# Layer 0 of a two-layer kernel: the queries join the seven products of half blocks, row sums come from DRAM, and the norm's unrotated weights move to the turned keys

## The chip, the cores and the metric

The kernel runs on one core of a Trainium2 chip. A core has five engines that each run their own instruction stream in order: TensorE (PE in the profile, with its weight loads as PEld), VectorE (DVE), ScalarE (ACT), GpSimd (POOL) and SyncE (SP, here only issuing transfers). The metric is the time of one execution on the device in microseconds. Before the change the median of three runs is 2171.02 us (2167.05 to 2172.69).

## The reference

The program is a small two-layer network on 4 sequences of 512 tokens with 512 features, all in 32-bit floats. Each layer normalises its input and adds an attention and a mixture of experts to it. The change concerns the attention of layer 0, which has 16 heads of 128 features:

```python
q = rope(rmsnorm(xn @ Wq + bq, qn_w))            # per head: 128 features
lk = rope(rmsnorm(xn @ Wlk + blk, kn_w))
lv = xn @ Wlv + blv
# sparse part: every 4 tokens are one compressed entry (ck, cv); top 8 of 128
sc = q @ ck.T * scale, causal;  ctx_sparse = softmax over the top 8 @ cv
# local part: window of 128 tokens back
ctx_local = softmax(q @ lk.T * scale, band) @ lv
out = merge_heads(0.5 * (ctx_sparse + ctx_local)) @ Wo + bo
```

`rmsnorm(x, w)` is `x * rsqrt(mean(x*x) + 1e-6) * w` over the 128 features of a head. `rope` rotates the first 64 features of a head by angles that depend on the token's place in its sequence, and leaves the other 64 as they are. The three products with `Wq`, `Wlk` and `Wlv` are each 2048 x 512 by 512 x 2048.

## The kernel before

**Loops.** The attention of layer 0 runs in 32 steps, written `for i, (g, b) in enumerate(steps)`: 8 groups `g` of two heads, and within each the 4 sequences `b`. Step i computes scores and context of its two heads, and between these it projects the queries, keys and values of step i + 1 (`project(i + 1)`). A step is 512 tokens, four blocks of 128 rows. Below these 32 steps are called loops 0 to 31. Loop 31 has nothing to project.

**Other work in the loops.** `run0((i, place))` lets other work in at five places of every loop: layernorm and routing in loops 0 to 4; the 39 expert blocks of layer 0 in loops 5 to 24 (`Experts.turn` transposes a block of gathered rows, tile `trm_r`, L382, with an ACT copy to `xT`, L384; `Experts.apply` multiplies it by the expert's weights, tile `hp_r`, L392, evicts on DVE, L394, and stores to DRAM, `yd`, through SP); the combination of the experts' rows in loops 24 to 28; the layernorm of layer 1 in loops 29 to 31.

**Projection.** Before the change the queries are plain products: `queries0(t)` (L554, tile `pq`) multiplies two row blocks by `Wq` in four steps of 128 features, 256 columns each. It is called twice a loop, for rows 0-255 and rows 256-511. Keys and values of the group together are one product of a 2 x 2 block matrix, computed by seven half-size products instead of eight (a Strassen form; `product`, L524, tile `p`): rows are split at 256, features at 256, and the outputs are keys and values. It needs sums of blocks of rows (`sums_x`, on DVE, tiles x1 to x3) and sums of weight blocks (`combine_weights`, once a group). `first_keys` makes p1 and p2, `second_keys` p6, p7 and p4, `values0` p5 and p3. Each product is a tile of 128 x 512 in PSUM: two row blocks of 256 columns.

**Norm and rotation.** `rope` (L427 to L448) runs on a block of 256 rows and 2 heads, that is four columns of sums `ss`, of queries or of keys. ACT squares and sums each of the four (L432), POOL adds epsilon (L434, L436) and raises to the power of -1/2 (L437), DVE rotates (L440 to L443), and for the queries ACT scales (L447, four copies). For the keys the scale is left to the exponential of the scores (`norm_k`, L613). `back()` turns the result with four PE transposes (tile `trq`, L543) and one ACT copy into `qkT` (L544). `t1` and `t2` hold cosines and sines times the norm weights, for all 128 features.

**Scores and context.** `scores` (L594 to L627) computes the sparse scores `sp` and local scores `st` on PE, the exponentials on ACT, the band mask on POOL (L617), and the top 8 on DVE. `turn` transposes the sparse weights (tile `trs`, L635, copies to `sT` on ACT, L637). `context` computes local and sparse context of one head into three PSUM tiles `ca`, `cb` and `cc` (L651, L653, L657), then on DVE the reciprocals of the sums (L660, L663), on ACT `half`, the sparse part scaled (L668, four copies), and on DVE `ctx`, the two parts added (L670, first from `cb`, then three from `ca`). `turn_context` (L677, L678) turns it into `cT`, and `output` (L685, L688) multiplies by `Wo` and adds to `acc`.

**PSUM.** `psum(tag, name)` gives banks of 128 x 512 floats in rotation: three for `mm` (projections, outputs, experts), three for `sc` (scores, context) and two for `tr` (transposes). A tile's first write waits until all reads of the bank's previous tile are done.

**Order.** The order in which the source states the work, and a scheduler that keeps each engine busy by its own estimates, set each engine's instruction order when the kernel is built. On the chip every engine runs its stream in that order. In loops 5 to 23 before the change PE runs: `op` of the loop before, scores of head 0, `pq`, p1 and p2, `trm_r`, scores of head 1, `trs`, `hp_r`, p6 and p7, `trq`, p4, `trq`, context of head 0, `trs`, `pq`, `trm_r`, `trq`, context of head 1, `trc`, `hp_r`, p5 and p3, `trq`, `trc`, `op`.

The loop's calls of the projection are these:

```python
back_q0, back_k0 = queries_a(), keys_a()
...
back_k1 = keys_b(back_q0)
ctx0 = context(i, 0, lT0, sT0, lv)
back_q1 = queries_b()
ctx1 = context(i, 1, lT1, sT1, lv)
values_()
```

Of the kernel before, what the change touches and what calls it, by code (L numbers as in the profile page):

```python
# [12 lines left out]
F32 = mybir.dt.float32  # L13
# [19 lines left out]
HG = 2  # L33
# [11 lines left out]
def two_layers(ctx: ExitStack, tc: tile.TileContext, a: dict, out: bass.AP, large: bass.AP):  # L45
# [29 lines left out]
    def load_group(g, between=None):  # L75
        cols = slice(g * HG * D, (g + 1) * HG * D)
        bqk = wpool.tile([P, 2, HG * D], F32, tag="bqk", name=f"bqk_{g}")
        bvg = wpool.tile([P, HG * D], F32, tag="bvg", name=f"bvg_{g}")
        ws = []
        for nm in ("Wq", "Wlk", "Wlv"):  # L80
            w = wpool.tile([P, KC, HG * D], F32, tag=nm, name=f"{nm}_{g}")
            nc.sync.dma_start(out=w, in_=a[nm][:, cols].rearrange("(k p) c -> p k c", p=P))
            ws.append(w)
            if nm == "Wq":
                for nm_, dst in (("bq", bqk[:, 0, :]), ("blk", bqk[:, 1, :]), ("blv", bvg)):
                    nc.sync.dma_start(out=dst, in_=a[nm_][cols].partition_broadcast(P))
            if between:
                between(nm)
        return ws, bqk, bvg
# [6 lines left out]
    def combine_weights(g):  # L96


        (_, w_k, w_v), bqk, bvg = groups[g]
        k1, k2, v1, v2 = w_k[:, 0:2, :], w_k[:, 2:4, :], w_v[:, 0:2, :], w_v[:, 2:4, :]  # L100
        t2_, t3_, t4_ = (wpool.tile([P, 2, HG * D], F32, tag=f"wT{x}", name=f"wT{x}_{g}", bufs=1) for x in (2, 3, 4))
        tc.keep_in_program_order(V.tensor_tensor(t3_, v2, v1, ALU.subtract))
        tc.keep_in_program_order(V.tensor_tensor(v1, v1, k1, ALU.subtract))
        tc.keep_in_program_order(V.tensor_tensor(t2_, v2, v1, ALU.subtract))
        tc.keep_in_program_order(V.tensor_tensor(t4_, t2_, k2, ALU.subtract))
        tc.keep_in_program_order(V.tensor_tensor(bvg, bvg, bqk[:, 1, :], ALU.subtract))
        sums_w[g] = t2_, t3_, t4_
# [14 lines left out]

    nw = wk0.tile([P, 2, D], F32, tag="s", name="nw")
    cos = wk0.tile([P, TC + 1, D], F32, tag="lT", name="cos")
    sin = wk0.tile([P, TC + 1, D // 2], F32, tag="lT", name="sin")

    def load_between(nm):
        if nm == "Wq":
            load_x(1)
        if nm == "Wlk":  # L130
            nc.sync.dma_start(out=nw[:, 0, :], in_=a["qn_w"].partition_broadcast(P))
            nc.sync.dma_start(out=nw[:, 1, :], in_=a["kn_w"].partition_broadcast(P))
            nc.sync.dma_start(out=cos, in_=a["c_cos"])
            nc.sync.dma_start(out=sin, in_=a["c_sin"])
            for n in range(2, TC):
                load_x(n)

    load_x(0)
    groups = {0: load_group(0, load_between)}
# [32 lines left out]
    t1 = const0.tile([P, TC + 1, 2, D], F32, tag="t1", name="t1")  # L172
    t2 = const0.tile([P, TC + 1, 2, D // 2], F32, tag="t2", name="t2")

    def tables():

        wmax = small.tile([P, 2], F32, tag="wmax", name="wmax")
        tc.keep_in_program_order(V.tensor_reduce(wmax, nw, AX.X, ALU.max, apply_absolute_value=True))
        V.tensor_tensor(wmax[:, 0:1], wmax[:, 0:1], wmax[:, 1:2], ALU.mult)
        V.tensor_scalar(wide, wmax[0:1, 0:1], LIMIT / math.sqrt(D), None, ALU.is_gt)  # L180


        for w in range(2):

            tc.keep_in_program_order(V.tensor_scalar(nw[:, w, :], nw[:, w, :], math.sqrt(D), None, ALU.mult))
            tc.keep_in_program_order(G.tensor_tensor(
                t1[:, :, w, :], cos, nw[:, w, :].unsqueeze(1).to_broadcast([P, TC + 1, D]), ALU.mult
            ))
            for half, other in ((0, 1), (1, 0)):
                G.tensor_tensor(  # L190
                    t2[:, :, w, ts(half, 32)],
                    sin[:, :, ts(half, 32)],
                    nw[:, w, ts(other, 32)].unsqueeze(1).to_broadcast([P, TC + 1, 32]),
                    ALU.mult,
                )
# [223 lines left out]
    lv = const0.tile([P, TC, HG, D + 1], F32, tag="lv", name="lv")  # L419
# [6 lines left out]
    def rope(qb, tt1, tt2, n, inner, pool, name, scale=True):  # L426


        sq = pool.tile([P, D], F32, tag="sq", name=f"sq_{name}", bufs=1)
        ss = small.tile([P, n], F32, tag="ss" if scale else "ssk", name=f"ss_{name}", bufs=3 if scale else 4)  # L430
        for h in range(n):
            A.activation(sq, qb[:, h, :], AF.Square, accum_out=ss[:, h : h + 1])  # L432
        if scale:
            G.tensor_scalar(ss, ss, D * 1e-6, None, ALU.add)  # L434
        else:
            G.tensor_scalar(ss, ss, D * 1e-6, float(D), ALU.add, ALU.mult)  # L436
        G.tensor_tensor(ss, ss, nhalf[:, 0:n], ALU.pow)  # L437
        r1 = pool.tile([P, n, D], F32, tag="r1", name=f"r1_{name}", bufs=2 if n > 1 else 1)
        r2 = pool.tile([P, n, D // 2], F32, tag="r2", name=f"r2_{name}", bufs=1)
        V.tensor_tensor(inner(r1), inner(qb), tt1, ALU.mult)  # L440
        V.tensor_tensor(inner(r2[:, :, 0:32]), inner(qb[:, :, 32:64]), tt2[0], ALU.mult)
        V.tensor_tensor(inner(r2[:, :, 32:64]), inner(qb[:, :, 0:32]), tt2[1], ALU.mult)
        V.tensor_tensor(r1[:, :, 0:64], r1[:, :, 0:64], r2, ALU.add)  # L443
        if not scale:
            return r1, ss
        for h in range(n):
            A.activation(r1[:, h, :], r1[:, h, :], AF.Copy, scale=ss[:, h : h + 1])  # L447
        return r1  # L448

    def compress(b, pool):  # L450
# [27 lines left out]
        for i, w in enumerate((wk, wv)):  # L478
            for k in range(KC):
# [5 lines left out]
        r = rope(ck, t1[:, TC, 1:2, :], (t2[:, TC, 1:2, 0:32], t2[:, TC, 1:2, 32:64]), 1,  # L485
                 lambda t: t, pool, f"ck_{b}")
        yield
        tr = psum("tr", f"trck_{b}")
        PE.transpose(tr[:, 0:C], r[:, 0, :], ident)
        A.copy(ckT[:, b, :], tr[:, 0:C])  # L490
# [7 lines left out]
    norm_k = {}  # L498

    def project(i):  # L500
# [4 lines left out]
        (w_q, w_k, w_v), bqk, bvg = groups[g]  # L505
        qkT = qp.tile([P, 2 * HG, S], F32, tag="qkT", name=f"qkT_{g}_{b}")
        x11, x12, x21, x22 = (xnT[:, ts(f, 2), ds(b * S + t * 256, 256)] for t in range(2) for f in range(2))
        half = [P, 2, 256]
        keep_ = {}

        def tmp(tag):
            keep_[tag] = wk0.tile(half, F32, tag=tag, name=f"{tag}_{i}", bufs=1)
            return keep_[tag]

        def sums_x():
            V.tensor_tensor(tmp("x3"), x11, x21, ALU.subtract)
            V.tensor_tensor(tmp("x1"), x21, x22, ALU.add)
            V.tensor_tensor(tmp("x2"), keep_["x1"], x11, ALU.subtract)

        def product(nm, x, w):  # L520
            p = psum("mm", f"{nm}_{i}").rearrange("p (c d) -> p c d", c=2)
            for c in range(2):
                for k in range(2):
                    PE.matmul(p[:, c, :], lhsT=x[:, k, ts(c, P)], rhs=w[:, k, :], start=(k == 0), stop=(k == 1))  # L524
            return p

        def finish(qb, w_, t):

            nm = f"{i}_{w_}_{t}"
            r = rope(  # L530
                qb.rearrange("p c (h d) -> p (c h) d", h=HG),
                t1[:, ts(t, 2), w_, :].unsqueeze(2).to_broadcast([P, 2, HG, D]),
                [t2[:, ts(t, 2), w_, ts(i_, 32)].unsqueeze(2).to_broadcast([P, 2, HG, 32]) for i_ in range(2)],
                2 * HG, lambda x: x.rearrange("p (c h) d -> p c h d", c=2), wk0, nm, scale=(w_ == 0),
            )
            if w_ == 1:
                r, norm_k[(i, t)] = r

            def back():
                tr = psum("tr", f"trq_{nm}")  # L540
                for h in range(HG):
                    for c in range(2):
                        PE.transpose(tr[:, ts(h * 2 + c, P)], r[:, c * HG + h, :], ident)  # L543
                A.copy(qkT[:, ts(w_, HG), ts(t, 256)], tr.rearrange("p (h t) -> p h t", h=HG))  # L544
            return back

        def rows_(nm):
            return wk0.tile(half, F32, tag="qb", name=f"qb_{nm}_{i}")

        def queries0(t):  # L550
            pq = psum("mm", f"pq_{i}_{t}").rearrange("p (c d) -> p c d", c=2)
            for c in range(2):
                for k in range(KC):
                    PE.matmul(pq[:, c, :], lhsT=xnT[:, k, ds(b * S + (2 * t + c) * P, P)], rhs=w_q[:, k, :],  # L554
                              start=(k == 0), stop=(k == KC - 1))
            qb = rows_(f"q{t}")
            V.tensor_tensor(qb, pq, bqk[:, 0, :].unsqueeze(1).to_broadcast(half), ALU.add)
            return finish(qb, 0, t)

        def first_keys():  # L560
# [1242 lines left out]
```

## Time and profile before

| | |
|---|---|
| median of three runs | 2171.02 us (2167.05 to 2172.69) |
| profiled execution | 2168.7 us |
| its span (first to last instruction) | 2166.8 us |
| granted TensorE clock, mean | 0.993 |
| PE, DVE, ACT, POOL busy | 2108.3, 1458.9, 848.4, 687.0 us |
| one loop with an expert (474 to 521 us) | 47.0 us |
| one loop without experts (1426.7 to 1467.7 us) | 41.0 us |

The profile is of one execution. Busy time is the time in which an engine runs at least one counted instruction. A line of a timeline gives start and duration in us, the engine, the line of the source, the operation, the tile written and those read, the shapes, and how many instructions the line joins; in brackets stand the idle time of the engine before it, and what ended it. A line of the chain of waits gives start, duration and what the run's end waited for at that time. A float32 matmul is two instructions in the profile: `x16` on L554 is eight products.

### The profile page before, as it was taken

How to read it: one execution, taken by the hardware profiler on the slowest of the kernel's cores; microseconds unless marked ns; L12 is line 12 of the kernel's file. 1: busy time of each engine (PE TensorE's matmuls, PEld its weight loads, DVE VectorE, ACT ScalarE, POOL GpSimd, SP SyncE). 2: the span in 40 equal slices, each digit the busy share in tenths (PEclk: the TensorE clock that was granted, in tenths of full speed). 3: DMA queues.
4: the chain of work that ended last, by engine and by line, in shares of the span. 5: the costliest groups of instructions: out<-in, count | busy, mean ns of one | idle time of the engine just before them, and what ended most of it. 6: DMA issues, size and time to landing. Idle time of an engine off the chain costs nothing.

```text
span 2166.8 us, 28936 instructions
## 1 busy us (share of the span) xinstructions
PE 2108.3 (97%) x9970; PEld 1392.0 (64%) x9970; DVE 1458.9 (67%) x3674; ACT 848.4 (39%) x2649; POOL 687.0 (32%) x725
## 2 busy tenths in 40 slices
PE   6999999999999999999999999999999999999998
PEld 5667877777777777777777887885334343443332
DVE  6868976666666766666666788885485444446775
ACT  3444444334444334444433444552333233333332
POOL 3212234343323323333323444443012222213430
PEclk9999999999999999999999999999999999999998
DMA  7001023322322332232232112102016566653321
GB/s 229 35 11 38 11 73 97 106 78 83 105 98 74 105 105 71 83 124 80 78 123 83 59 50 63 35 30 92 10 69 209 203 227 209 205 198 117 107 83 41
DMA packets 70813, 211.24 MB, mean 97 GB/s; under 512 B 8449, under 2 KB 25857, under 8 KB 60673
## 3 DMA queue, kind: packets, MB, share of 16 engines
q0 software_dynamic: 22592, 139.47, 19.2%
q1 hardware_dynamic: 45760, 65.63, 9.4%
q10 hardware_dynamic: 2304, 4.20, 0.5%
q8 instruction: 81, 1.33, 0.3%
q14 instruction: 76, 0.61, 0.1%
HBM read 176.24 MB, written 33.03 MB: 97 GB/s over the span
## 4 chain that ended last, share of the span: by engine, by line
PE 68%; issue 13%; DVE 8%; POOL 5%; DMA 3%; ACT 3%; SPq 0%; POOLq 0%; ACTq 0%; DVEq 0%
PE p L524 15%; PE pq L554 9%; PE op L685 9%; PE hp_r L392 7%; PE st L609 4%; PE sp L600 2%; PE trq L543 2%; PE qp L905 2%; POOL we_r L375 2%; PE ca L653 2%; PE o L976 1%; DVE pS L936 1%; PE st L916 1%; DMA row_r<-yd,slot_r 1%; PE cc L657 1%
## 5 line engine op out<-in xcount | busy, mean ns | idle before, releaser
L392 PE MATMUL hp_r<-we_r,xT_r 128*128 128x512 f32 x624 | 283.4, 597 | 4.3 <-DMA we_r<-in_ewx,wrow_r 4.2
L617 POOL TENSOR_TENSOR lT<-lT,lmask 128x512 f32<-128x512 f32 (+1 forms) x128 | 151.2, 1196 | 318.6 <-ACT lT L613 318.6
L554 PE MATMUL pq<-Wq,xnT 128*128 128x256 f32 x1024 | 234.0, 381 | 1.2 <-DVE u L570 1.2
L685 PE MATMUL op<-Wo,cT 128*128 128x512 f32 x512 | 230.5, 599 | 2.1 <-DVE lv L587 2.1
L554 PEld LDWEIGHTS pq<-Wq,xnT 128*128 128x128 f32 x1024 | 190.2, 191 | 24.9 <-DVE u L570 1.5
L392 PEld LDWEIGHTS hp_r<-we_r,xT_r 128*128 128x128 f32 x624 | 115.1, 191 | 139.4 <-issue 129.6
L373 POOL DMA_INDIRECT xr_r<-xnd,rows_r x78 | 83.6, 1072 | 330.9 <-PE trm_r L382 232.9
L613 ACT ACTIVATE lT<-st,ss 128x256 f32<-128x256 f32 (+1 forms) x256 | 96.8, 443 | 234.2 <-PE st L609 234.1
L544 ACT COPY qkT<-trq 128x512 f32<-128x512 f32 x128 | 74.7, 583 | 231.6 <-PE trq L543 231.2
L685 PEld LDWEIGHTS op<-Wo,cT 128*128 128x128 f32 x512 | 91.7, 190 | 113.8 <-issue 82.3
L918 ACT ACTIVATE pT<-st 128x1024 f32<-128x1024 f32 x128 | 123.8, 1019 | 70.1 <-PE st L916 54.5
L437 POOL TENSOR_TENSOR ss<-ss,nhalf 128x4 f32<-128x4 f32 x128 | 144.5, 1129 | 10.7
L384 ACT COPY xT_r<-trm_r 128x512 f32<-128x512 f32 x78 | 45.2, 580 | 260.6 <-PE trm_r L382 203.0
L688 DVE TENSOR_TENSOR acc<-acc,op 128x512 f32<-128x512 f32 x128 | 87.5, 684 | 80.7 <-PE op L685 80.5
L394 DVE TENSOR_TENSOR yr_r<-hp_r,we_r 128x512 f32<-128x512 f32 x78 | 53.7, 688 | 116.5 <-PE hp_r L392 116.5
L447 ACT ACTIVATE r<-r,ss 128x128 f32<-128x128 f32 x256 | 81.9, 390 | 105.8 <-POOL ss L437 103.4
L524 PE MATMUL p<-Wlv,x 128*128 128x256 f32 x512 | 117.5, 380 | 0.0
L524 PE MATMUL p<-Wlk,xnT 128*128 128x256 f32 x512 | 117.4, 383 | 0.0
L524 PE MATMUL p<-wT,x 128*128 128x256 f32 x512 | 117.4, 380 | 0.0
L407 POOL DMA_INDIRECT row_r<-yd,slot_r x64 | 75.3, 1176 | 120.1 <-DVE row_r L1008 53.6
L524 PEld LDWEIGHTS p<-wT,x 128*128 128x128 f32 x512 | 95.9, 190 | 23.8 <-issue 12.1
L524 PEld LDWEIGHTS p<-Wlv,x 128*128 128x128 f32 x512 | 95.5, 190 | 20.7 <-issue 9.1
(253 smaller groups left out, 4394.4 us busy)
## 6 DMA issues: line engine op xcount, KB each, us to landing
yd<-yr_r SPq DMA_DIRECT2D x78, 256.0 KB, 2.4
acc<-in_x SPq DMA_DIRECT2D x16, 256.0 KB, 5.1
Wq<-in_Wq SPq DMA_DIRECT2D x8, 512.0 KB, 3.7
Wlk<-in_Wlk SPq DMA_DIRECT2D x8, 512.0 KB, 3.6
xnd<-xn ACTq DMA_DIRECT2D x16, 256.0 KB, 2.6
Wlv<-in_Wlv SPq DMA_DIRECT2D x8, 512.0 KB, 9.1
Wo<-in_Wo SPq DMA_DIRECT2D x8, 512.0 KB, 3.6
xnd<-xn SPq DMA_DIRECT2D x16, 256.0 KB, 2.0
```

What stands on the lines that cost most here:

```text
L373: G.indirect_dma_start(out=x, out_offset=None, in_=xnd, in_offset=at_rows(self.r.rows[:, i : i + 1]))
L392: PE.matmul(hp, lhsT=xT[:, k, :], rhs=w[:, ts(k, HID)], start=(k == 0), stop=(k == KC - 1))
L437: G.tensor_tensor(ss, ss, nhalf[:, 0:n], ALU.pow)
L447: A.activation(r1[:, h, :], r1[:, h, :], AF.Copy, scale=ss[:, h : h + 1])
L524: PE.matmul(p[:, c, :], lhsT=x[:, k, ts(c, P)], rhs=w[:, k, :], start=(k == 0), stop=(k == 1))
L554: PE.matmul(pq[:, c, :], lhsT=xnT[:, k, ds(b * S + (2 * t + c) * P, P)], rhs=w_q[:, k, :], start=(k == 0), stop=(k == KC - 1))
L609: PE.matmul(st[:, ds((t % 2) * 256, n)], lhsT=qkT[:, HG + h, ts(t, P)], rhs=qkT[:, h, ds(t * P, n)], start=True, stop=True)
L613: A.activation(lT[:, ds(half * 512 + c * 256, n)], st[:, ds(c * 256, n)], AF.Exp, scale=norm_k[(i, half)][:, c * HG + h : c * HG + h + 1])
L617: G.tensor_tensor(dst, dst, lmask.rearrange("p a w j -> p (a w j)")[:, 0:n], ALU.mult)
L685: PE.matmul(op, lhsT=cT[:, h, ts(t, P)], rhs=wo[:, h, :], start=(h == 0), stop=(h == HG - 1))
L688: V.tensor_tensor(acc[:, n, :], acc[:, n, :], op, ALU.add)
L918: A.activation(pt[:, ts(pair, 2), :], st, AF.Exp, scale=SCALE1)
```

## The change

- The queries join the seven products. The weights come regrouped: `wA` holds for each group the two heads' queries and head 0's keys (384 columns), `wB` the two heads' values and head 1's keys (384 columns). `product` now makes one 128-row half (c = 0, 1) into its own PSUM tile of 128 x 384, so a projection is 14 tiles; each is evicted by DVE by itself.
- The calls are `first` (p1, p2), `second` (p6, p7, then p4) and `third` (p5, p3) instead of two query halves and three key and value parts. The source calls `second` ahead of head 0's context, nothing of the projection between the two contexts, and `third` behind head 1's context.
- `rope` is split into `squares` and `rotate`. `finish(t)` runs both on six blocks at once (q0, q1, k0 for two row blocks), and scales the four query blocks in place by ACT copies. `rotate` treats only the 64 rotated features, in place, so its last step waits for the squares to have read them.
- The norm weights of the 64 unrotated features go into `turned`, a factor per feature: `turn_keys` and the compressed keys' copy scale by it when keys are turned. `t1` and `t2` hold 64 features; there are twelve table operations on POOL in place of six.
- Head 1's keys are kept beside the values in `lv[:, :, 2]`, normed and rotated in `third`, and turned at the start of the next loop (`turn_last(1)`).
- Sums of rows: computed in the first projections of the four sequences, stored to DRAM (`xsd`), and for the later projections (i >= 4) loaded by four transfers of 256 KB per projection (`load_sums`).
- `qkT` has one buffer instead of two.

```diff
+    def load_sums(i):
+        for n in range(4):
+            xs[n] = wk0.tile([P, 2, 256], F32, tag=f"x{n}", name=f"x{n}_{i}", bufs=1)
+            if i >= B:
+                nc.sync.dma_start(out=xs[n].rearrange("p k t -> p (k t)"), in_=xsd[steps[i][1], n])
...
+        def product(nm, x, w, c):
+            p = psum("mm", f"{nm}_{i}_{c}")[:, 0 : 3 * D]
+            for k in range(2):
+                PE.matmul(p, lhsT=x[:, k, ts(c, P)], rhs=w[:, k, :], start=(k == 0), stop=(k == 1))
+            return p
...
+        def finish(t):
+            x = qb[t].rearrange("p c (h d) -> p (c h) d", d=D)
+            sq[t] = squares(x, 6, wk0, f"{i}_{t}", float(D))
+            by = lambda tt: tt[:, ts(t, 2), :, :].rearrange("p c h d -> p (c h) d")
+            rotate(x, by(t1), by(t2), 6, wk0, f"{i}_{t}")
+            for j in (0, 1, 3, 4):
+                A.activation(x[:, j, :], x[:, j, :], AF.Copy, scale=sq[t][:, j : j + 1])
...
+        def turn_keys(h):
+            tr = psum("tr", f"trk_{i}_{h}")
+            for t in range(TC):
+                PE.transpose(tr[:, ts(t, P)], lv[:, t, 2, 0:D] if h else qb[t // 2][:, t % 2, ts(2, D)], ident)
+            A.activation(qkT[:, HG + h, :], tr, AF.Copy, scale=turned[:, 0:1])
...
+        def second(between):
+            u2, u3 = u["u2"], tmp("u3")
+            t2_, t3_, t4_ = sums_w[g]
+            for c in range(2):
+                V.tensor_tensor(u2[:, c, :], product("p6", xs1, t2_, c), u2[:, c, :], ALU.add)
+                V.tensor_tensor(u3[:, c, :], product("p7", xs2, t3_, c), u2[:, c, :], ALU.add)
+            between()
+            qb[1] = wk0.tile(rows3, F32, tag="qb", name=f"qb1_{i}")
+            for c in range(2):
+                V.tensor_tensor(qb[1][:, c, :], u3[:, c, :], product("p4", x22, t4_, c), ALU.subtract)
+            finish(1)
...
-        em0, lT0 = scores(i, 0, qkT)
-        back_q0, back_k0 = queries_a(), keys_a()
-        sums_x()
+        em0, lT0 = scores(i, 0, now)
+        turn_last(1)
+        if more:
+            load_sums(i + 1)
+            qkT, sums_x, first, second, third, turn_queries, turn_keys = project(i + 1)
+            first()
+            sums_x()
         run0((i, 0))
...
-        back_k1 = keys_b(back_q0)
-        back_k0()
+        if more:
+            second(lambda: turn_queries(0))
         ctx0 = context(i, 0, lT0, sT0, lv)
         sT1 = turn(i, 1, em1)
-        back_q1 = queries_b()
...
         ctx1 = context(i, 1, lT1, sT1, lv)
         turn_context(i, 0, ctx0, cT)
+        if more:
+            turn_queries(1)
         run0((i, 3))
-        values_()
-        back_q1()
+        if more:
+            turn_keys(0)
+            third()
         turn_context(i, 1, ctx1, cT)
```

More of the change, by code (lines that the diff above doesn't have):

```diff
@@ L96, in combine_weights @@
     def combine_weights(g):
[L99 to L106, printed above, removed]
+        (w_a, w_b), b2 = groups[g]
+        a2, b1, b2_ = w_a[:, 2:4, :], w_b[:, 0:2, :], w_b[:, 2:4, :]
+        t2_, t3_, t4_ = (wpool.tile([P, 2, 3 * D], F32, tag=f"wT{x}", name=f"wT{x}_{g}", bufs=1) for x in (2, 3, 4))
+        for o, x, y in ((t3_, b2_, b1), (b1, b1, w_a[:, 0:2, :]), (t2_, b2_, b1), (t4_, t2_, a2),
+                        (b2[:, 1, :], b2[:, 1, :], b2[:, 0, :])):
+            tc.keep_in_program_order(V.tensor_tensor(o, x, y, ALU.subtract))
         sums_w[g] = t2_, t3_, t4_
@@ L120, in load_x, with load_between @@
         nc.sync.dma_start(out=acc[:, n, :], in_=x_v[:, n, :])
+    xsd = dram.tile([B, 4, P, 512], F32, tag="xsd", name="xsd")
+    R = D // 2
     nw = wk0.tile([P, 2, D], F32, tag="s", name="nw")
[L124 to L133, printed above, removed]
+    cs_ = wk0.tile([P, 2, TC + 1, R], F32, tag="lT", name="cs")
+    cos, sin = cs_[:, 0], cs_[:, 1]
+    turned = const0.tile([P, 1], F32, tag="turned", name="turned")
+    wcol = small.tile([P, 2], F32, tag="wcol", name="wcol", bufs=1)
+    def load_between(nm, f):
+        if nm == "wA" and f == 1:
+            for w, src in enumerate(("qn_w", "kn_w")):
+                nc.sync.dma_start(out=nw[:, w, :], in_=a[src].partition_broadcast(P))
+                nc.sync.dma_start(out=wcol[:, w : w + 1], in_=a[src].rearrange("(d o) -> d o", o=1))
+            nc.sync.dma_start(out=cos, in_=a["c_cos"][:, :, 0:R])
             nc.sync.dma_start(out=sin, in_=a["c_sin"])
@@ L547, in rows_ @@
[L547 to L551, printed above, removed]
-            for c in range(2):
[L553 to L558, printed above, removed]
@@ L589, in project @@
-        return qkT, (sums_x, lambda: queries0(0), first_keys, second_keys, lambda: queries0(1), values0)
+        rows3 = [P, 2, 3 * D]
+        u, qb, sq = {}, {}, {}
+        def sums_x():
+            if i < B:
+                V.tensor_tensor(xs[2], x11, x21, ALU.subtract)
+                V.tensor_tensor(xs[0], x21, x22, ALU.add)
+                V.tensor_tensor(xs[1], xs[0], x11, ALU.subtract)
+                V.tensor_tensor(xs[3], x12, xs[1], ALU.subtract)
+                for n in range(4):
+                    nc.sync.dma_start(out=xsd[b, n], in_=xs[n].rearrange("p k t -> p (k t)"))
@@ new lines, in third @@
+        def third():
+            u2, u3 = u["u2"], u["u3"]
+            u5 = wk0.tile(rows3, F32, tag="qb", name=f"u5_{i}")
+            by_head = lambda x: x.rearrange("p c (h d) -> p c h d", d=D)
+            for c in range(2):
+                V.tensor_tensor(u5[:, c, :], product("p5", xs0, w_b[:, 0:2, :], c), b2[:, 1, :], ALU.add)
+            V.tensor_tensor(lv[:, 2:4, :, 0:D], by_head(u3), by_head(u5), ALU.add)
+            V.tensor_tensor(u2, u2, u5, ALU.add)
+            for c in range(2):
+                p3 = product("p3", xs3, w_b[:, 2:4, :], c).rearrange("p (h d) -> p h d", d=D)
+                V.tensor_tensor(lv[:, c, :, 0:D], p3, by_head(u2)[:, c], ALU.add)
+            x = lv[:, :, 2, 0:D]
+            ss = squares(x, TC, wk0, f"{i}_k", float(D))
+            rotate(x, t1[:, :, 2, :], t2[:, :, 2, :], TC, wk0, f"{i}_k")
+            for h in range(HG):
+                norm_k[(i, h)] = [ss[:, t : t + 1] if h else sq[t // 2][:, ds(t % 2 * 3 + 2, 1)] for t in range(TC)]
@@ L591, in scores @@
+        xs0, xs1, xs2, xs3 = (xs[n] for n in range(4))
+        return qkT, sums_x, first, second, third, turn_queries, turn_keys
     def scores(i, h, qkT):
@@ L793, in two_layers @@
     run0 = schedule(jobs0)
-    qkT, parts_ = project(0)
+    load_sums(0)
+    qkT, sums_x, first, second, third, turn_queries, turn_keys = project(0)
     start_sequence(0)
```

202 lines of the change are left out of this document (78 added, 124 removed).

## The prediction

> **What bounds the kernel now.** I read the page first: the busy shares, the slices, the chain of waits.
>
> ```profile
> PE 2108.3 (97%) x9970; PEld 1392.0 (64%) x9970; DVE 1458.9 (67%) x3674; ACT 848.4 (39%) x2649; POOL 687.0 (32%) x725
> ...
> PE   6999999999999999999999999999999999999998
> ```
>
> TensorE (PE) is busy 97% of the span and nearly full in every slice but the first. So matmul time taken out shortens the run, unless PE then waits. Next I read the chain inside one loop of layer 0 that carries an expert (474 to 521 us). Columns: start, duration, what.
>
> ```profile
> 500.91 1.73 PE p L524 x8
> 502.64 0.44 PE trq L543 x4
> 503.07 0.23 PE ca L653 x2
> ...
> 505.08 0.45 PE cc L657 x4
> 505.53 0.44 PE trs L635 x4
> 505.97 3.46 PE pq L554 x16
> 509.42 0.44 PE trm_r L382 x4
> 509.86 0.44 PE trq L543 x4
> 510.30 0.23 PE ca L653 x2
> ```
>
> Each piece starts where the one before ends: PE waits for nothing. The reader should look at what stands between the context of head 0 (503.07 to 505.53) and that of head 1 (from 510.30): 4.77 us, of which 3.46 us is the second half of the queries. Head 1's `ca` needs a PSUM bank of tag sc that head 0's context still holds; it comes free when DVE has made ctx from it, and ctx needs ACT's `half`. That chain runs in those 4.77 us. Its length without cover shows in the last loop, which projects nothing (timelines of PE, ACT and DVE):
>
> ```profile
> 1485.49 0.62 ACT L668 ACTIVATE half<-cb,sums 128x128 f32<-128x128 f32 x2 [0.44 <-DVE sums L663]
> ```
> ```profile
> 1486.15 0.35 DVE L670 SCALAR_TENSOR_TENSOR ctx<-cb,sums,half 128x128 f32<-128x128 f32 x1 [0.77 <-ACT half L668]
> ```
> ```profile
> 1486.65 0.46 PE L653 MATMUL ca<-lv,lT 128*128 128x129 f32 x2 [0.49 <-DVE ctx L670]
> ```
>
> There PE idles for ctx, and from the start of `half` to `ca` is 1486.65 − 1485.49 = 1.16 us. Last, the ACT timeline for what a block of queries costs there:
>
> ```profile
> 487.60 0.31 ACT L432 ACTIVATE sq<-qb_q 128x128 f32<-128x128 f32 x1 [0.59 <-DVE qb_q L557]
> ...
> 489.12 0.19 ACT L432 ACTIVATION_READ_ACCUMULATOR sq<-qb_q 128x1 f32 x1
> 490.88 1.28 ACT L447 ACTIVATE r<-r,ss 128x128 f32<-128x128 f32 x4 [1.58 <-POOL ss L437]
> 492.07 0.56 ACT L384 COPY xT_r<-trm_r 128x512 f32<-128x512 f32 x1
> ```
>
> Squares of one head every 0.43 us; 1.57 us (489.31 to 490.88) for POOL's add and power on four columns; four scaling copies in 1.19 us. ACT runs in its written order: what stands behind the copies waits with it.
>
> **The change, part by part.** The profiled execution took 2168.7 us, its span 2166.8. It is 2.3 us under the median of 2171.0; I add the sum to both.
>
> *Matmul time.* Removed in each of 31 projections: two `pq` groups of 16 and seven `p` groups of 8, 88 instructions of 256 columns at 3.455/16 = 0.216 us: 19.0 us. Added: 56 instructions of 384 columns. No row has 384; it lies between 0.216 (256) and 0.430 to 0.4375 (512: `hp_r` 3.44/8, `op` 7.00/16), half-way 0.323 to 0.327: 18.1 to 18.3 us. I take 18.1, since `hp_r`, like these products, comes in unbroken groups. Gain 0.9 us a loop (0.7 at the least); transposes stay at eight query and eight key transposes a projection.
>
> *What moves.* By the instruction orders, PE now has in loops 5 to 23: p6 and p7, the first queries' transposes, p4 for both 128-row halves, context of head 0, trs (0.44), trm_r (0.44), context of head 1. The 3.46 us of queries are gone from the gap, and so is a trq. On ACT, `half` of head 0 stands behind six squares of qb1 (q0, q1, k0 by two row halves) and four scaling copies of qb1. Before, only four squares of keys stood there; their result was first needed much later. The copies wait for the power, that for the squares, those for DVE's eviction of p4. From the end of p4's second half:
> - eviction of 128x384 between 128x256 (0.42) and 128x512 (0.685): 0.55, and 0.04 hand-over: 0.59
> - three squares of that half (the other three run during it): 3 x 0.434 = 1.30
> - POOL: 1.57 with four columns. One column takes 0.58, four 1.04, so 0.15 a column, two more 0.31: 1.88
> - four copies 1.19: `half` starts at 4.96
> - to `ca` of head 1: 1.16, so 6.12.
>
> PE's cover is context 2.46 + trs 0.44 + trm_r 0.44 = 3.34. **New stall: 6.12 − 3.34 = 2.8 us a loop.** Lower end: power no dearer with six (−0.31), eviction as 256 columns (−0.13): 2.3. Upper: power at its mean of 1.13, not 1.04, and 0.18 a column (+0.15), eviction as 512 (+0.13), copies by busy time (+0.09): 3.15. Behind the waiting `ca` stands the rest of PE's queue; behind `half` on ACT stand the copies of sT (0.66) and of the expert's xT (0.56). With `half` taking about 1.25 these end near 6.9 and 7.4; PE reads sT 1.6 after `ca` begins (7.7) and needs xT's bank 2.9 after (9.0), so they cost nothing more.
>
> The Trainium skill, GPSIMD Engine Reference, § 3.1 Elementwise, states about 2.6 cycles an element for a two-input operation, so two more columns would cost nothing there. By an estimate from that page the stall would be 2.5, and the sum about 7 us lower. This trace's row (0.58 to 1.04 for one to four columns) says otherwise and carries my number.
>
> *Other loops.* In 24 to 28 the order pulls p5 into the gap and has no trm_r: cover 4.83, stall 1.3, plus 0.2 for the turned ctx at the tail (row: from trc at 1489.18 to its successor at 1491.56 2.38, cover 2.17). 29 and 30: cover 4.63, stall 1.5. Loop 3: cover 5.5, stall 0.6. Loops 0 to 2: cover 7.7 or more, no stall. Loop 4: p4 lies after head 0's context, no stall.
>
> *Sums of rows.* DVE drops three or four 128x512 sums a loop from loop 4 on; with half-width rotation and the extra evictions it gains some 2 us a loop, worth nothing since PE bounds (the windows give DVE 30.4 of 47 us). In exchange SP issues four loads of 256 KB a loop, 28 MB in all. They are issued a whole loop (47 us) before their reader; a 256 KB transfer lands in 2.4 (yd) to 5.1 us (in_x), and the 16 DMA engines are busy 0.23 to 0.29 in these windows. They stand behind the weight loads on SP, which are issued a loop or more ahead too. Cost 0; if that cover were gone, up to 5 us a loop. SP's yd store waits for the expert's result and holds the loads behind it, by less than a loop.
>
> *Unrotated norm weights, keys' head 1.* Scaling now rides on the copies that turn the keys (one ACT copy each as before). Head 1's keys are finished at the tail and turned behind head 0's scores of the next loop; needed there about 10 us later, covered. Smaller tables at the start: twelve POOL operations for six, but half as wide: within ±3 us of PE's start (PE is busy 43 of the first 60 us).
>
> *Sum.* Loops 5 to 23: 19 x (2.8 − 0.9) = +36. Loops 24 to 28: 5 x (1.5 − 0.9) = +3. Loops 29, 30: 2 x 0.6 = +1. Loops 0 to 4: 0.6 − 5 x 0.9 = −4. Total +36: 2204.7 against the profiled execution, **2207** against the median. With the ends: 26 stalls shorter by 0.45 gives 2195; longer by 0.35 and a gain of 0.7 instead of 0.9 gives 2222.
>
> **Rivals.**
> 1. *No stall: `half` isn't held.* For it: ACT is busy only 39%, the scheduler may run copies elsewhere, and before, in the same loop, `half` of head 1 waited behind copies at no cost to PE. Against: that one had 7 us of cover, and the order has `half` behind the copies in all 19 loops. Price: 31 x 0.9 = −28: 2143. It decides where the stall falls under 28/19 = 1.5 us, that is if `half` starts 1.3 us earlier than reckoned. Chance 0.09.
> 2. *Half a stall.* The first copies or squares slip under p4, or the context gets later: 1.2 to 2 us a loop, 2168 to 2183. Chance 0.07.
> 3. *The clock falls too.* PE idled 3.34 us before 21.75, and the granted clock in the window after was 0.67; a wait of 2.12 us before another window left it at 1.00:
>
> ```profile
> 22.20:27.40 5.20, 5.20 (x19) 4.19 (x18) 4.88 (x10) 2.20 (x9) 1.51 (x3) 0.67 0.66 197
> 30.10:33.60 3.50, 3.49 (x8) 0.65 (x8) 3.50 (x9) 1.47 (x8) 1.21 (x2) 1.00 1.05 388
> ```
>
> (columns: window, length, busy PE, PEld, DVE, ACT, POOL, clock, DMA share, GB/s). A stall of 2.8 lies between the two, nearer the upper. One such fall costs 5.20 x 0.33 = 1.7 us; 19 of them +32: 2239. Against: 2.8 is under 3.34, and the loop is otherwise full. Chance 0.08.
> The Trainium skill, TensorE: Matmul & The Clock Gate, Part 1 (What's actually happening), states that a free-running window of about 3.4 us spent idle halves the clock; by that page this stall wouldn't drop it, and the sum would stay as it is.
> 4. *More waits elsewhere*: the sums land late, or the tail's keys: 0.5 to 1 us a loop, 2222 to 2236. For it: the DMA bytes; against: a loop of cover. Chance 0.08.
>
> **How the numbers follow.** The likeliest case, the stall of 2.8, has 0.68 (2195 to 2222). 2207 is its time. Leaving out rival 1 and the lower part of rival 2 below (0.13) and most of rival 3 above (0.06) gives 2180 to 2237. The measurement can tell 0.3%, 6.5 us: faster is under 2164.5, rival 1 and a little of 2: 0.10; same to 2177.5: 0.04; slower 0.86.
>
> **What would show it.** Right: in a loop of 5 to 23, PE's `ca` of head 1 with some 2.8 us idle before it, released by DVE ctx; ACT's copies of qb1 right before `half`, released by the power; that power of six columns near 1.35 us; clock 1.00; a period near 49 us; loops 0 to 2 shorter by 0.9. Product instructions of 0.32 us show the gain. Wrong: `half` starting before the copies, a PE gap at p6 or p7 released by a DMA, or at st released by the turned keys.

## The result, and the profile after

The changed kernel takes 2268.9 us (median of four runs, 2267.26 to 2269.65); the kernel before 2170.1 (four runs, 2167.05 to 2172.69). The ratio is 1.0455, with a 95% interval of 1.0437 to 1.0473. That is 98.8 us slower, where 36 were forecast and 2237 was the upper end of the range. The sign was right, and so was the wait that was named; the size was not.

Busy shares of the changed kernel, its slices and its chain of waits, as the profile gives them:

```profile
PE 2122.8 (94%) x8946; PEld 1234.0 (54%) x8946; DVE 1444.6 (64%) x3596; ACT 867.2 (38%) x2649; POOL 674.0 (30%) x667
...
PE   7999899999989999999999998899999999999998
...
PE 61%; issue 13%; DVE 9%; ACT 7%; POOL 6%; DMA 3%; SPq 0%; POOLq 0%; ACTq 0%; DVEq 0%
```

PE has lost 3 points of busy share. Before, the chain had PE at 68% and ACT at 3%; now PE has 61% and ACT 7%. What PE waited for says where (engine, line, what ended the wait; total in us, times, the longest):

```profile
PE ca L666 <- DVE ctx L683: 71.6, 25, 3.4
PE p L536 <- DVE u L576: 13.4, 7, 3.1
```

Before, the same kind of wait before `ca` came to 0.5 us in all. Two windows that cover the same 18 loops (6 to 23), first of before, then of after (window, length, busy time of PE, PEld, DVE, ACT and POOL, granted clock, DMA share, GB/s):

```profile
339.87:1185.51 845.64, 845.64 (x4250) 652.64 (x4249) 561.03 (x1519) 352.87 (x1296) 284.73 (x300) 1.00 0.28 93
```
```profile
346.38:1257.12 910.74, 855.26 (x3674) 570.66 (x3673) 559.18 (x1465) 363.79 (x1296) 277.44 (x264) 0.97 0.32 107
```

Before, PE was busy in every one of the 845.64 us. After, it idles 55.5 us (18 times 3.08). And its busy time is 855.26, longer than before, although it runs 576 fewer instructions and the matmuls were to get shorter. The clock column gives the reason: 0.97. Starts of `sp`, one after the other, show two kinds of loop: 15 of the 18 take 50.87 us, the other three 49.22. The chain through loop 9 (start, duration, what) has both losses:

```profile
519.49 1.31 PE p L536 x4
...
520.82 0.57 DVE qb L581
...
523.63 0.41 ACT sq L440 x2
524.04 0.09 issue
524.13 0.56 POOL ss L441
...
524.77 1.37 POOL ss L442
...
526.47 0.97 ACT qb L550 x3
527.44 0.52 ACT half L681 x2
527.96 0.02 issue
527.98 0.36 DVE ctx L683
528.34 0.14 issue
528.48 0.46 PE ca L666 x2
...
530.56 0.86 PE cb L670 x4
531.42 0.86 PE cc L670 x4
```

The chain leaves PE at p4, runs through eviction, squares, POOL, the copies of `qb` and `half`, and comes back to PE at `ca` of head 1, as the prediction has it. Then `cb` x4 takes 0.86 us, where it took 0.45 before: for a while TensorE runs at half its rate. Here are windows around this wait and around that of loop 10, whose period is 49.22:

```profile
525.40:529.80 4.40, 1.32 (x12) 1.35 (x13) 1.13 (x4) 3.32 (x12) 1.78 (x2) 1.00 0.21 60
529.80:533.20 3.40, 3.40 (x19) 3.40 (x18) 0.68 (x4) 0.37 (x2) 0.00 (x0) 0.51 0.00 0
576.28:579.36 3.08, 0.01 (x1) 0.04 (x1) 0.50 (x2) 2.32 (x9) 1.80 (x2) 1.00 0.15 21
579.40:582.80 3.40, 3.40 (x31) 3.40 (x32) 3.40 (x9) 1.24 (x5) 0.00 (x0) 1.00 0.14 57
```

In loop 9 the 3.4 us behind the wait have a clock of 0.51 and hold 19 matmul records; in loop 10 the same wait, 3.08 us long, is followed by a clock of 1.00 and 31 records.

The difference by place, from starts of first instructions in the two traces:

| stretch | before, us | after, us | difference | predicted |
|---|---|---|---|---|
| to loop 0's first scores | 61.16 | 64.00 | +2.8 | 0 ± 3 |
| loops 0 to 5 | 278.7 | 282.4 | +3.7 | −2 |
| loops 6 to 23 | 845.6 | 910.7 | +65.1 | +34 |
| loop 24 to layer 1's first product | 314.7 | 343.4 | +28.7 | +4 |
| layer 1 | 666.6 | 665.0 | −1.6 | 0 |
| span | 2166.8 | 2265.5 | +98.7 | +36 |

In loops 6 to 23: 18 x 3.08 of waiting are 55.4; 15 windows of 3.41 us at half the clock, of which each loses 1.65 (50.87 − 49.22), are 24.8; the shorter matmuls give back the rest, 15.1, or 0.84 a loop.

### The profile page after: what moved, and what is told of

It reads as the page before. It is cut to its first block, busy times and chain, and to the rows that moved or that the text cites. A ratio compares the mean times of both kernels' runs of the same rounds, so it can differ in the third digit from the quotient of the medians.

```text
span 2265.5 us, 27315 instructions
## 1 busy us (share of the span) xinstructions
PE 2122.8 (94%) x8946; PEld 1234.0 (54%) x8946; DVE 1444.6 (64%) x3596; ACT 867.2 (38%) x2649; POOL 674.0 (30%) x667
## 4 chain that ended last, share of the span: by engine, by line
PE 61%; issue 13%; DVE 9%; ACT 7%; POOL 6%; DMA 3%; SPq 0%; POOLq 0%; ACTq 0%; DVEq 0%
PE p L536 20%; PE op L698 10%; PE hp_r L400 6%; PE st L622 4%; ACT sq L440 4%; PE qp L920 2%; PE sp L613 2%; POOL ss L442 2%; DMA row_r<-yd,slot_r 2%; POOL we_r L383 2%; PE ca L666 1%; PE o L991 1%; ACT qb L550 1%; PE st L931 1%; PE po L1041 1%
## 5 line engine op out<-in xcount | busy, mean ns | idle before, releaser
L536 PE MATMUL p<-wT,x 128*128 128x384 f32 x512 | 174.2, 489 | 5.6 <-DVE u L576 4.8
L536 PE MATMUL p<-wB,x 128*128 128x384 f32 x512 | 176.7, 488 | 0.5 <-DVE u L589 0.5
L536 PE MATMUL p<-wA,xnT 128*128 128x384 f32 x512 | 174.0, 492 | 2.8 <-DVE u L568 1.6
L440 ACT ACTIVATE sq<-qb 128x128 f32<-128x128 f32 x384 | 118.9, 310 | 126.4 <-DVE qb L581 59.8
L666 PE MATMUL ca<-lv,lT 128*128 128x129 f32 x384 | 83.9, 303 | 72.1 <-DVE ctx L683 71.6
L536 PEld LDWEIGHTS p<-wA,xnT 128*128 128x128 f32 x512 | 95.7, 193 | 64.8 <-DVE u L568 2.9
L441 POOL TENSOR_SCALAR ss<-ss 128x6 f32<-128x6 f32 x64 | 35.0, 546 | 294.8 <-ACT sq L440 294.8
L536 PEld LDWEIGHTS p<-wB,x 128*128 128x128 f32 x512 | 92.5, 191 | 52.9 <-DVE u L589 1.6
L550 ACT ACTIVATE qb<-qb,ss 128x128 f32<-128x128 f32 x256 | 81.8, 390 | 101.3 <-POOL ss L442 97.3
L666 PEld LDWEIGHTS ca<-lv,lT 128*128 128x128 f32 x384 | 67.0, 211 | 89.2 <-issue 81.3
```

The source lines that it names most:

```text
L440: A.activation(sq, x[:, h, :], AF.Square, accum_out=ss[:, h : h + 1])
L536: PE.matmul(p, lhsT=x[:, k, ts(c, P)], rhs=w[:, k, :], start=(k == 0), stop=(k == 1))
L550: A.activation(x[:, j, :], x[:, j, :], AF.Copy, scale=sq[t][:, j : j + 1])
L666: PE.matmul(loc[t], lhsT=lT[:, ds(t * 256, P)], rhs=lv[:, t, h, :], start=(t == 0), stop=True)
```

## The experiments

All are edits of the changed kernel, and each ratio is to the kernel before on the same chip (medians near 2169 to 2170). The edits are shown in excerpts.

**1. The copies behind `half`.** The four scaling copies of the second query block are stated later, and pinned there; those of the first block are pinned where they stood.

```diff
-            for j in (0, 1, 3, 4):
-                A.activation(x[:, j, :], x[:, j, :], AF.Copy, scale=sq[t][:, j : j + 1])
+            if t == 0 or i == 0:
+                scale(t)      # scale(t) holds the four copies, pinned in program order
...
         sT1 = turn(i, 1, em1)
+        if more:
+            scale(1)
```

> The four scaling copies of the second query block stand on ACT behind half and the copies of sT of head 0, instead of ahead of half; nothing else changes in the order of PE. My theory (half held by the copies makes the 3.08 us wait, and the wait makes the clock fall): half starts about 0.55 after cc, the wait before ca of head 1 falls from 3.08 to about 0.85 us, the clock stays at 1.00 in loops 6 to 23, their period goes from 50.87 (49.22 without a fall) to about 47.0, 18 loops save 65 us, and the run takes about 2195 us (2185 to 2205). Rival, the loads of the sums of rows or the longer squares set the wait: period and time stay near 2269. Rival, the clock falls for another reason: periods near 48.7, about 2225.

Measured: 2179.9 us, ratio 1.0042 (1.0028 to 1.0056), below the forecast range. The period is 47.00 in nearly all of loops 6 to 23, and the clock stays at 1.00. The window over these loops, then ACT and PE of loop 9 in this kernel:

```profile
338.57:1184.83 846.26, 830.61 (x3673) 546.00 (x3672) 559.91 (x1465) 363.44 (x1296) 278.51 (x264) 1.00 0.33 115
```
```profile
505.66 0.62 ACT L686 ACTIVATE half<-cb,sums 128x128 f32<-128x128 f32 x2 [1.06 <-DVE sums L681]
506.17 0.63 ACT L686 ACTIVATE half<-cc,sums 128x128 f32<-128x128 f32 x2
506.67 0.66 ACT L655 COPY sT<-trs 32x128 f32<-32x128 f32 x3
507.24 1.27 ACT L555 ACTIVATE qb<-qb,ss 128x128 f32<-128x128 f32 x4
```
```profile
506.82 0.46 PE L671 MATMUL ca<-lv,lT 128*128 128x129 f32 x2 [0.85 <-POOL ss L442]
```

`half` now waits for its own sums alone, the copies come last, and the wait is the 0.85 us that was expected. (Its releaser is put down to POOL, which is the last event of several; the copies of `qb`, which need that power, start only at 507.24, after `ca`.) Loops 6 to 23 became 64.5 us shorter, as forecast. The time fell 15 us further than that forecast, since loops 24 to 31 became 17 us shorter (their waits before `ca` fell from 13.0 to 3.5 us in all, their time at half the clock from 20.5 to 6.8) and loops 0 to 5 became 8 us shorter. So the order on ACT is what made the wait: PE runs the same order in loops 6 to 23, and no size was changed.

**2. The wait filled with useless work.** Two products whose result nobody reads stand in the wait.

```diff
+        if 5 <= i < 24:
+            idle_ = psum("mm", f"idle_{i}")
+            for _ in range(2):
+                tc.keep_in_program_order(
+                    PE.matmul(idle_[:, 0 : 3 * D], lhsT=ident, rhs=groups[g][0][0][:, 0, :], start=True, stop=True))
         ctx1 = context(i, 1, lT1, sT1, lv)
```

> In loops 5 to 23 two products of 384 columns (1.29 us on PE) whose result is used by nobody stand between trm_r and ca of head 1, inside the wait. My theory: the wait's end stays where it is, PE's idle time falls from 3.08 to 1.79 us, which is under the about 2 us in a window of 3.41 us after which the clock fell, so the clock stays at 1.00 in loops 6 to 23, every period is 49.22, 15 loops save 1.65 us, and the run takes about 2244 us: more work and less time. Rival, the low clock doesn't come from this idle time: no change, 2269, or longer by 19 x 1.29 = 24 if PE isn't idle for the reason given.

Measured: 2246.0 us, ratio 1.0356 (1.0338 to 1.0373): 23 us less than the changed kernel, with more work. The wait in loop 9 and the window over loops 6 to 23:

```profile
519.54 1.46 PE L864 MATMUL idle<-wA,ident 128*128 128x384 f32 x4
522.78 0.46 PE L666 MATMUL ca<-lv,lT 128*128 128x129 f32 x2 [1.78 <-DVE ctx L683]
```
```profile
345.63:1231.56 885.93, 853.88 (x3746) 557.69 (x3744) 558.62 (x1465) 363.42 (x1296) 277.21 (x264) 1.00 0.32 110
```

All 18 periods are 49.21 to 49.23, and the clock is 1.00. The fall of the clock is due to PE's idle time, and it is a cost beside the wait: 24.8 us in these loops.

**3. The wait filled half as much.** One product (0.65 us) instead of two.

```diff
-            for _ in range(2):
+            for _ in range(1):
```

> As the filled wait, with one product (0.65 us) instead of two: PE idles 2.43 us in loops 5 to 23. My theory (the clock halves for a window of 3.41 us if PE idled some 2.0 us or more of the window before, in a grid that runs on by itself): the idle time still reaches 2.0 us in one window in about four loops of five, the periods are 49.2 and 50.9 as without the fill, and the time stays near 2269. Rival, the fall grows smoothly with idle time: a period half-way, about 2257.

Measured in one run: 2267.2 us. The wait in loop 9 and the window over loops 6 to 23:

```profile
526.43 0.54 PE L666 MATMUL ca<-lv,lT 128*128 128x129 f32 x2 [2.43 <-DVE ctx L683]
```
```profile
345.97:1256.71 910.74, 866.93 (x3709) 575.52 (x3708) 559.40 (x1465) 363.85 (x1296) 277.48 (x264) 0.97 0.31 107
```

PE idles 2.43 us in each loop, 15 of the 18 periods are 50.86 to 50.89, and three 49.22 or 49.23, as in the changed kernel. With 0.64 us less of idle time nothing is gained, with 1.29 less the whole 24.8 us. So in these loops the price of idling goes up in a step, between 1.78 and 2.43 us.

**4. p4 between the contexts.** `second` is cut in two; the part from p4 on is called behind `turn(i, 1, em1)`, and `turn_queries(1)` behind the expert's product.

```diff
+        def fourth():          # p4, its evictions, finish(1)
...
         sT1 = turn(i, 1, em1)
+        if more:
+            fourth()
...
-        if more:
-            turn_queries(1)
         run0((i, 3))
         if more:
+            turn_queries(1)
             turn_keys(0)
```

> p4 and what follows it (evictions, squares, rotation, scaling copies of the second block) are moved between the two contexts, and the second queries are turned behind the expert's product. My theory: p4 covers half and ctx of head 0 (2.58 + 0.88 us of cover for about 1.7 us), the copies come behind half, no wait and no fall of the clock in loops 6 to 23, period 46.98 - 0.84 = 46.14, 18 loops save 80 us against the changed kernel; with the loops from 24 on about as they are now, 2180 us (2160 to 2190). Rival, the 384-column products or the loads leave a loss of their own: periods above 47, time above 2200.

Measured: 2180.6 us, ratio 1.0049 (1.0032 to 1.0066), as forecast; the period is 46.63 instead of 46.14, since PE now waits 0.5 us in most loops before the turned keys of head 0: their bank is released by the copy of cT, and that stands on ACT behind the same four copies (`trk` here is the transpose of the keys):

```profile
PE trk L562 <- ACT cT L695: 7.6, 14, 0.8
```

In loops 25 to 28, which have no expert's product to cover the copies, the second queries' transposes wait 2.9 to 3.2 us for them.

**5. The second queries turned later still.** As 4, but behind p5, the keys of head 0 ahead of it (shown against 4).

```diff
-            turn_queries(1)
             turn_keys(0)
-            third()
+            third(lambda: turn_queries(1))      # called between p5 and p3
```

> As with p4 between the contexts, and the second queries are turned behind p5 and the turned keys of head 0 ahead of it. The 0.5 us that PE waits for the copy of cT in each of loops 6 to 23 is covered by p5 (2.58 us), their period falls from 46.64 to 46.14 (9 us together), and the waits of the turned queries in loops 25 to 28 (2.9 us each, where no expert's product covers the copies) go as well (10 to 13 us): 2158 us (2150 to 2166). If what is left is queueing on ACT that moves on to the next reader, 2175 to 2180.

Measured: 2172.3 us, ratio 1.0016 (1.0006 to 1.0027), above the forecast range and below the 2175 to 2180 of the other case. Thirteen of the loops 6 to 23 have 46.0 us and no wait. In the other five (6, 10, 14, 18 and 22) DVE sums the next group's weights between the contexts; evictions come late and 1.4 us are lost, 1.8 the first time. Loops 25 to 28 gained less than forecast: PE's long wait became three shorter ones (turned keys, turned queries, `op`).

**6. Sums of rows on DVE.** No loads from DRAM.

```diff
-            if i >= B:
+            if False:
                 nc.sync.dma_start(out=xs[n].rearrange("p k t -> p (k t)"), in_=xsd[steps[i][1], n])
...
-            if i < B:
+            if True:
                 V.tensor_tensor(xs[2], x11, x21, ALU.subtract)
```

> Sums of rows are computed on DVE for every projection, as before the change, and nothing is loaded from DRAM; the rest is the changed kernel. My theory: the loads cost nothing in loops 6 to 23, where the period stays 50.87 or 49.22; the run stays within 1% of 2269, a few us more or less in loops 24 to 30, where DVE is busier. Rival, the 28 MB of loads cause the loss: back to 2210 or less.

Measured: 2259.6 us, ratio 1.0423 (1.0400 to 1.0446). A window over 18 loops, from head 1's first scores in loop 6 to those in loop 24:

```profile
357.53:1269.65 912.12, 856.67 (x3674) 569.10 (x3673) 592.71 (x1538) 367.75 (x1296) 273.35 (x264) 0.97 0.26 87
```

912.12 against 910.74 us: the loads cost nothing here, nor do DVE's 34 us of extra work. What is gained lies in loops 24 to 31 (335.8 us instead of 349.9, counted from the last context of loop 23 to that of loop 31); loops 0 to 5 take 4.4 us longer. In loops 24 to 31 the order came out differently: in loop 25 a gather stands on POOL ahead of the power of six columns instead of behind it.

**7. The additions behind `second`.** In loops 24 to 28 the experts' rows are gathered by POOL and added on DVE. The chain in loop 25 of the changed kernel:

```profile
1312.34 0.81 POOL ss L442
...
1314.05 2.61 POOL lT L630 x2
1316.66 0.16 issue
1316.82 4.49 DMA row_r<-yd,slot_r
1321.32 0.03 issue
1321.34 0.75 DVE acc L708
1322.09 0.48 DVE u L576
```

The gather is issued behind the power and behind head 1's masks; its rows land 4.49 us later; DVE's addition waits for it, and behind the addition on DVE stands the eviction of p6, for which PE waits 3.10 us. The edit states the job behind `second` in loops 25 to 31:

```diff
-        run0((i, 1))
+        if i < 25:
+            run0((i, 1))
         if more:
             second(lambda: turn_queries(0))
+        if i >= 25:
+            run0((i, 1))
```

> In loops 25 to 31 of the changed kernel the jobs of place 1 (the gathered rows' additions among them) are stated behind second instead of ahead of it, so that on DVE the additions stand behind the evictions of p6 and p7. My theory for the loss in these loops (POOL issues a gather behind the power of six columns and head 1's masks, it lands 4.5 us later, DVE's addition waits for it, and p6's evictions queue behind that addition): the four waits of PE for the eviction of p6 (3.1, 1.2, 3.1, 1.2 us) go, and with them up to three windows of low clock (1.7 us each); loops 24 to 31 get 8 to 13 us shorter, the run takes about 2259 us; the waits before ca of head 1 stay. Rival, DVE's load or the transfers themselves set these waits: they stay, 2269.

Measured: 2249.5 us, ratio 1.0367 (1.0343 to 1.0391). The waits for p6 in loops 25 to 28 go, save one of 0.45; from the end of head 1's context in loop 23 to that in loop 31 it is 330.5 us instead of 349.9. That is 19.4, more than the 8 to 13 expected. PE's idle time in this stretch fell from 28.5 to 17.8 us. Time at half the clock fell from 20.5 to 4.5 us, and half of that difference is 8.0. The waits before `ca` hardly changed in sum (13.0 to 11.9 us); the longest fell from 3.4 to 1.9, but loop 25 now has one too.

**8. Both edits, 5 and 7.**

```diff
+            fourth()                            # behind turn(i, 1, em1)
...
+            third(lambda: turn_queries(1))
...
+        if i >= 25:
+            run0((i, 1))                        # behind second
```

> The two edits together: p4 between the contexts with late queries, and in loops 25 to 31 the additions behind second. Theory: 2155 us (2146 to 2163), below the kernel before by the 0.84 us a loop that the seven products save (26 us), less what the additions still hold up. Rival: a loss of 10 us or more stays in loops 24 to 31 and the time is at or above 2165.

Measured: 2167.8 us, ratio 0.9985 (0.9971 to 0.9999), above the forecast range and where the rival had it: loops 24 to 31 still took 332.3 us, against 318.9 before the change. PE still idles 21.4 us there, at full clock throughout.

**9. Each where it fits.** p4 between the contexts up to loop 23; from 24 on p4 ahead of them as in the changed kernel, with copies behind `half` and additions behind `second`; the next group's weights combined behind head 1's turned context.

```diff
+            if i >= 24:
+                fourth()
...
+        if more and i >= 24:
+            scale(1)
...
-        if b == 2 and g + 1 in groups:
-            combine_weights(g + 1)
...
         turn_context(i, 1, ctx1, cT)
+        if b == 2 and g + 1 in groups:
+            combine_weights(g + 1)
```

> Up to loop 23 as with p4 between the contexts and late queries; from loop 24 on p4 ahead of head 0's context as in the changed kernel, but its scaling copies pinned behind half, and the additions behind second; the weights of the next group are combined behind head 1's turned context instead of between the contexts. Theory: loops 0 to 23 end near 1146 us (the 1.4 us that DVE's weight sums cost in loops 7, 11, 15, 19 and 23 go: 7 us), loops 24 to 31 take about 320 us (330.5 with the additions behind alone, less the waits before ca of head 1), layer 1 as before: 2150 us (2142 to 2160), clearly under the kernel before. Rival: what is taken out of loops 24 to 31 comes back as another wait, or the weight sums hold up the tail: 2160 to 2170.

Measured: 2156.3 us (six runs, 2153.16 to 2158.28), ratio 0.9940 (0.9928 to 0.9953): 0.6% below the kernel before. Its loops 6 to 23:

```profile
332.96:1161.12 828.16, 828.16 (x3674) 542.30 (x3673) 550.22 (x1465) 361.30 (x1296) 286.67 (x264) 1.00 0.34 118
```

PE is busy in all 828.16 us, 17.5 less than before: 0.97 a loop is what the seven products are worth. The 1.4 us that the weight sums had cost in each of five loops (6, 10, 14, 18 and 22, not those that the expectation names) are gone. Loops 24 to 31 took 332.4 us, not the 320 expected. The chain of this kernel in loop 25 has what is left:

```profile
1229.38 4.15 DMA row_r<-yd,slot_r
...
1233.62 0.75 DVE acc L720
1234.37 0.15 DVE sums L685 x2
...
1234.86 1.14 ACT half L693 x4
1236.01 0.48 ACT cT L703
1236.49 0.04 issue
1236.53 0.67 PE trk L569 x2
```

The addition has moved on to stand before head 1's sums; `half` and the copy of cT wait for those, and PE waits 2.78 us for the bank. Such waits, of 2.7 to 3.5 us, stand in each of loops 25 to 28, and each is followed by 3.4 us at half the clock. A gather is still late, one reader further on. This was not mended.

## Why the prediction was right or wrong

**Right: the bound and the wait.** PE was the bound, and removing the queries from the gap uncovered the chain over ACT. The wait before `ca` is in all of loops 5 to 23, released by DVE ctx, with the copies of `qb` right before `half`. Experiment 1 shows that their place is the cause, and experiment 6 that the loads, part of rival 4, are not.

**Its size: 3.08 for 2.78.** Terms of the sum, in loop 9: eviction 0.58 (0.59 forecast); squares, from there to the last one's end at 524.04, 1.39 (1.30); POOL 2.12 (1.88), with the add of six columns 0.56 where four had taken 0.33, and the power 1.37 (1.35 forecast); copies 1.19 (1.19); `half` to `ca` 1.13 (1.16). The cover was 3.33 (3.34). So POOL's add, which was left at its four-column price, is most of the 0.3 us that were missed; over 18 loops that is 5.4 us. The power's mean is 1402 ns on 128x6 and 1067 ns on 128x4 in the trace after. The Trainium skill, GPSIMD Engine Reference, § 3.1 Elementwise, states about 2.6 cycles an element for a two-input operation; by an estimate from that, the two further columns would cost next to nothing. The measurement differs, and it decides.

**The gain: 0.97 a loop in experiment 9, 0.84 in the changed kernel's loops without a fall of the clock.** An instruction of 384 columns takes 5.16/16 = 0.3225 us in the chain after, between 256 and 512 as interpolated (0.323).

**Wrong: rival 3 was left at a chance of 0.08.** The failing step is "2.8 is under 3.34, and the loop is otherwise full": it took the two rows (3.34 us of idle time followed by 0.67, 2.12 by 1.00) for a scale of unbroken idle time. What decides here is how much of the wait falls into one stretch of a fixed grid (see the last section), so a 3.08 us wait brings the clock down in 15 of 18 loops. Read that way the two rows agree with it: in the trace before, the grid cuts the wait of 3.34 us into 1.14 and 2.21, and the wait of 2.12 us into 1.79 and 0.32. The price that the rival gave (1.7 us each) was right: 1.65 was measured. Experiments 2 and 3 show both the cause and the step. This term is 24.8 of the 31 us by which loops 6 to 23 were missed.

**Wrong: "24 to 28: cover 4.83, stall 1.3".** The sum had +4 for everything from loop 24 on; it is +28.7. The stalls themselves came out near the forecast in sum: the waits before `ca` in loops 24 to 30 are 13.0 us, against 5 x 1.3 + 2 x 1.5 = 9.5. What the step left out are PE's waits for the eviction of p6, 10.5 us in loops 25 to 30, and 20.5 us at half the clock. In loops 25 to 28 that eviction stands on DVE behind an addition of gathered rows, which waits for its gather. In loop 25 of the trace before, gathers stand behind a power and a mask on POOL too (at 1246.42 us), but DVE reaches the additions that use them (1256.08 us) only behind the eviction of p4, and without a wait. Rival 4, "more waits elsewhere", named the loads and the keys as sources, not this one. Experiment 7 takes 19.4 us away by the place of these jobs alone.

**Smaller: the start and loops 0 to 5.** +6.5 us against −2. PE's idle time in loops 0 to 5 grew from 9.2 to 17.7 us. A wait of 2.9 us for p6's eviction in loop 4, where the routing is worked out, was not foreseen; no run separates these terms, and their cause stays open.

The reading of the sums' loads, the turned keys and SP's queue as costing nothing held in loops 6 to 23: experiment 9 has PE busy without a gap there, with all of them in place.

## What to carry to other kernels

Where an engine runs gapless, look at what each block of work covers before moving it: the 3.46 us of queries were not only work, they hid a chain of eviction, squares, power, copies and `half` that is 6 us long. Ask of each queue what is stated ahead of the instruction that releases the bank, as four copies nobody needed yet held it here, and put work that waits for a long chain behind work that is ready. And price a new idle time on TensorE twice, once for itself and once for the clock: in loops 6 to 23 that was 55.4 and 24.8 us.

## What the runs showed of the hardware

The granted clock halves for stretches of 3.413 us (or a few of them in a row) that lie on a grid that runs on by itself: their starts in the trace are whole multiples of 3.413 us apart. Sorting the waits of loops 6 to 23 in the changed kernel by how much of them falls into one stretch of that grid:

| largest part of the wait in one stretch, us | loops | clock in the next stretch |
|---|---|---|
| 2.03 to 3.09 | 15 | 0.5 |
| 1.71 to 1.94 | 3 | 1.0 |

A wait of 3.08 us that the grid cuts into 1.37 and 1.71 costs 3.08 us; cut into 0.72 and 2.36 it costs 4.73. In all ten traces of the changed kernel and its edits, between 290 and 1590 us, a stretch at full clock with 2.03 us or more of idle time was always followed by half the clock, one with less than 1.85 never; between 1.85 and 2.03 both happened. Outside that part of the run this limit does not hold: in the changed kernel, stretches with 1.60 us (from 41.8 us) and 1.70 us of idle time (from 1792.8 us, in layer 1) were followed by half the clock, and in experiment 1 one with 1.26 us (from 1701.0 us). No run here shows what sets the limit there. The Trainium skill, TensorE: Matmul & The Clock Gate, Part 1 (What's actually happening), has a free-running window of some 3.4 us and asks for a whole window spent idle. These rows confirm the window; here about 2.0 us of idle time in one of them were enough, and the measurement decides.
